# Left sums and weight sums of the second output projection as lanes of their own, ahead of the bias on VectorE

## The chip, the cores and the metric

The kernel runs on one core of a Trainium2 chip. The metric is the device time of one execution in microseconds; the time before is the median of 3 runs, 702.26 us (702.02 to 705.12). TensorE is PE in the profile, VectorE DVE, ScalarE ACT, GpSimd POOL; SP issues most transfers.

## The reference, cut to what matters

One decoder block in float32 on x of 2 x 512 x 1024 (two batches): causal attention with 32 query heads and 8 key heads, a product with a fake-quantised context, and a routed low-rank FFN, each with a layer norm in front and a residual around it.

```python
x = x + attn(layernorm(x))      # ... @ w_o.T + b_o, w_o 1024 x 1024
x = x + matmul(fake_quant(layernorm(x)), fake_quant(ctx))   # per batch, ctx 1024 x 1024
x = x + ffn(layernorm(x))       # x @ W_org.T + sum over e of coeff[e] * (x @ down[e]) @ up[e]
```

The change is in `out @ w_o.T + b_o` and the residual of the second batch.

## The kernel before

The whole kernel is one stream per engine, in the order in which the Python code records instructions. A program part is a generator: it records a few matmuls, yields, and in between `dispatch` lets VectorE and ScalarE record small steps ("hops") that wait in `lanes`. `dispatch` goes through the lanes by sorted name, so that a lane whose name begins with a lower number goes first, and takes a hop when its engine is not more than 0.6 us ahead of TensorE by a model of the clocks, and its inputs will be there. `force(key)` takes hops until the one with that key has been recorded. A recorded order is final: each engine runs its instructions in it and waits for what is not there yet.

The first part is attention for 2 batches x 8 groups of heads. Its pools (keys, queries, probabilities, and the PSUM banks of scores) are closed after the last group (`attn.close()`), and the space is given to a pool `tail` for the rest. Tiles of `tail` can be written once attention's last reader is done, which is the multiplication `oT` (L871) of the last group on VectorE.

At this point the rest begins: the four x tiles of batch 1 are loaded again (L273, 512 KB each, on SP), and a bias lane (4, "bias") adds b_o to each (L678, 128 x 1024).

The output projection of batch 1 is made by seven half-size products in place of eight, a Winograd form (`by_quarters`). With A the attention's output, B the weights wo, each cut into quarters, the products are called by numbers and run in the order 2, 1, 5, 6, 3, 7, 4:

- products 2 and 1 use quarters of A and B as they are. Product 2 is recorded beforehand, in the last steps of attention (`second_product`).
- product 5 is left sum `s_[0]` by the first weight sums `to1`; 6 is `s_[1]` by the second, `to2`; 3, 7 and 4 use later sums.
- the left sums are in a tile S (128 x 2 x 4 x 256): `s_[0]` = A(1,0) + A(1,1) and `s_[1]` = `s_[0]` - A(0,0) (`left_sums`, two instructions of 128 x 1024). After product 5 `s_[0]` is overwritten, after 6 `s_[1]`.
- the weight sums come from `right_sums`: four lists (first to fourth) of 4 instructions of 128 x 512 each, one for every k.

Each product is 2 PSUM banks of 4 matmuls of 128 x 512 in float32, which the profile counts as 16. What VectorE does with a result is `add` (L1335, x<-x,wo) and `gather` (L1253). `hooks` name what is to be recorded after a product.

Before the change, `left_sums` is the first hook of `rows_by_quarters`, so it is recorded when the projection starts; the weight sums are put in lane (1, "to") at the same place, in `output_by_quarters`. In the recorded order the four bias adds stand between `oT` and S.

What follows the projection of batch 1: `quantize_rows` (statistics L368, xn_b and a_b on ScalarE, L1026 and L1033), the transposes ta of a_b on TensorE (L1072), the base product of the FFN (wb, L1316, with sums tb and S again), cs (L958) and the context product ct (L969) of batch 1. Beside them the context of batch 1 is loaded in two buffers raw (L887), scaled on ScalarE (L910), bounded on VectorE (L914) and rounded on ScalarE (L918); the next load into a buffer is issued after the rounding. SP also issues the loads worg of the base weights (L1634) into the slots that wo's products have left. The last row tile of batch 0 runs in the same stretch: ct (L969, added at L975), st_c and xn_c (L368, L377), and its transposes tr_c on TensorE (L385).

Of the kernel before, what the change touches and what calls it, by code (L numbers as in the profile page):

```python
# [9 lines left out]
F32 = mybir.dt.float32  # L10
BF16 = mybir.dt.bfloat16
AF = mybir.ActivationFunctionType
ALU = mybir.AluOpType
AX = mybir.AxisListType

P = 128
B, S, D = 2, 512, 1024
# [5 lines left out]
NK = D // P  # L23
# [184 lines left out]
def kernel(  # L208
# [20 lines left out]
    nc = tc.nc  # L229
# [16 lines left out]
    def pool(name, bufs, on=stack, **kw):  # L246
        return Pool(on.enter_context(tc.tile_pool(name=name, bufs=bufs, **kw)), name, bufs)
# [5 lines left out]
    act = pool("act", 2)  # L253
# [18 lines left out]
    def load_x(dst, i):  # L272
        nc.sync.dma_start(dst, x[i * P : (i + 1) * P, :])  # L273
# [144 lines left out]
    def lane(name, *hops):  # L418
        lanes.setdefault(name, []).extend(hops)

    def take(name):
        hop = lanes[name].pop(0)
        if not lanes[name]:
            del lanes[name]
        hop.go()
# [17 lines left out]
    def force(key):  # L443
        while key not in done:
            name = next(n for n in sorted(lanes) if any(h.key == key for h in lanes[n]))
            hop = lanes[name][0]
            if hop.can and not hop.can():
                name = next(n for n in sorted(lanes) if not lanes[n][0].can or lanes[n][0].can())
            take(name)
# [54 lines left out]
    def take_xn():  # L504
        assert xn_free[0] > 0
        xn_free[0] -= 1

    def give_xn():
        xn_free[0] += 1
# [3 lines left out]
    xT, kTs, vs, qTs, wo = {}, {}, {}, {}, []  # L513
# [87 lines left out]
    def load_bo(name):  # L601
        t = xnp.tile([P, D], F32, tag="xn", name=name)
        nc.scalar.dma_start(t, bo.broadcast_to([P, D]))
        return t
# [72 lines left out]
    def add_bo(xi, bo_sb):  # L677
        nc.vector.tensor_tensor(xi, xi, bo_sb, ALU.add)  # L678

    def bias_lane(b, x_tiles, load):  # L680

        got = []

        def begin():
            take_xn()
            got.append(load())

        def add(t):
            add_bo(x_tiles[t], got[0])
            if t == NT - 1:  # L690
                give_xn()

        lane((4, "bias"), Hop("Activation", begin, can=lambda: xn_free[0] > 0))
        for t in range(NT):
            lane(
                (4, "bias"),
                Hop("DVE", lambda t=t: add(t), lambda t=t: [got[0], x_tiles[t]], key=("bias", b, t)),
            )
# [22 lines left out]
    stats, mT, invs, pts, oT = {}, {}, {}, {}, {}  # L721
# [446 lines left out]
    def load(key, deps, fn, chunks):  # L1168
        def run():
            w[key[0]] = fn()  # L1170
            made[key] = lambda: [w[key[0]](k) for k in range(chunks)]
            return iter(())

        unit(key, deps, run)
# [19 lines left out]
    sums = {}  # L1194
# [5 lines left out]
    def minus_(out_, a_, b_):  # L1200
        nc.vector.tensor_tensor(out_, a_, b_, ALU.subtract)

    def right_sums(quarter, shape, n, name):

        made = {}

        def of(t, k):
            return made[t][k // 2][:, k % 2, :]

        def two(t):  # L1210
            made[t] = [tail["t"](shape, f"{name}{t}_{i}") for i in range((n + 1) // 2)]

        def first(k):
            if k == 0:
                two(1)
            minus_(of(1, k), quarter(0, 1, k), quarter(0, 0, k))

        def second(k):
            if k == 0:
                two(2)  # L1220
            minus_(of(2, k), quarter(1, 1, k), of(1, k))

        def third(k):
            minus_(quarter(0, 1, k), quarter(1, 1, k), quarter(0, 1, k))

        def fourth(k):
            if k == 0:
                two(4)
            minus_(of(4, k), quarter(1, 0, k), of(2, k))

        makers = [[lambda k=k, f=f: f(k) for k in range(n)] for f in (first, second, third, fourth)]
        return makers, lambda t: lambda k: of(t, k)
# [71 lines left out]
    def left_sums(s_, a_):  # L1304
        nc.vector.tensor_tensor(s_[0], a_(1, 0), a_(1, 1), ALU.add)
        minus_(s_[1], s_[0], a_(0, 0))
        if len(s_) == 3:
            minus_(s_[2], a_(0, 0), a_(1, 0))

    def rows_product(name, b):  # L1310
        def product(p, l, r):
            n = NK // 2
            ps = [mm([P, 512], f"{name}{p}_{b}_{i}") for i in range(2)]
            for i in range(2):
                for k in range(n):
                    nc.tensor.matmul(  # L1316
                        ps[i], l[:, k, i * P : (i + 1) * P], r(k), start=(k == 0), stop=(k == n - 1)
                    )
                    yield 0.86
            return ps  # L1320

        return product

    def rows_by_quarters(name, b, lhs, weight, t_, hooks, ps2=None):


        n = NK // 2
        a_ = lambda i, j: lhs[:, (1 - j) * n : (2 - j) * n, i * 256 : (i + 1) * 256]
        b_ = lambda i, j: lambda k: weight((1 - i) * n + k)[:, j * 512 : (j + 1) * 512]

        product = rows_product(name, b)

        def add(i, j, h, src, first):
            xh = xs[b][2 * i + h][:, j * 512 : (j + 1) * 512]
            nc.vector.tensor_tensor(xh, xh, src, ALU.add)  # L1335

        if "S" not in sums:
            sums["S"] = act.tile([P, 2, n, 256], F32, tag="half", name="S")
        s_ = [sums["S"][:, i, :, :] for i in range(2)]
        more = tail["more"]([P, 2, 512], f"more{name}{b}")  # L1340
        hooks[0] = [lambda: left_sums(s_, a_)] + hooks.get(0, [])
        yield from by_quarters(product, a_, b_, s_, t_, [more[:, i, :] for i in range(2)], add, hooks, ps2=ps2)

    sums = {}
# [169 lines left out]
    def place_of(b):  # L1514

        if b:
            return lambda k: True
        return lambda k: ("v1" if k < 4 else ("k", 1, 1)) in done
# [4 lines left out]
    second_product = []  # L1523
# [86 lines left out]
    for t in range(NT):  # L1610
        xi = tail_x([P, D], f"x1_{t}")
        load_x(xi, NT + t)
        xs[1].append(xi)
    bias_lane(1, xs[1], lambda: load_bo("bo1"))
    rest = units[:]
    units.clear()
# [9 lines left out]
    def rows_quantised(i):  # L1626
        for t in (2 * i, 2 * i + 1):
            quantize_rows(1, t)

    def org_rows(i):  # L1630

        for k in range(i * NK // 2, (i + 1) * NK // 2):
            wk_ = ring_b([P, D], f"worg{k}")
            nc.sync.dma_start(wk_, worgT[k * P : (k + 1) * P, :])  # L1634
            org.append(wk_)

    def quarters_of(weight):
        return lambda i, j, k: weight((1 - i) * NK // 2 + k)[:, j * 512 : (j + 1) * 512]

    org = []  # L1640
    org_sums = []

    def sums_lane(makers, name, sources):

        for i, fns in enumerate(makers):
            for k, fn in enumerate(fns):
                key = {"key": (name, i)} if k == len(fns) - 1 else {}
                lane((1 if name == "to" else 2, name), Hop("DVE", fn, lambda k=k: sources(k), **key))

    def output_by_quarters():  # L1650
        of = quarters_of(lambda k: wo[k])
        makers, t_ = right_sums(of, [P, 2, 512], NK // 2, "to")
        sums_lane(makers, "to", lambda k: ())
        raws = [tail["raw"]([P, D], f"raw{i}") for i in range(2)]
        load_ctx(1, raws, place_of(1), lambda: None)
        hooks = {
            2: [lambda: force(("to", 0))],
            1: [lambda: force(("to", 0))],
            5: [lambda: force(("to", 1))],
            3: [lambda: rows_quantised(0), lambda: force(("to", 2)), lambda: org_rows(0)],  # L1660
            7: [lambda: force(("to", 3)), lambda: org_rows(1)],
            4: [lambda: rows_quantised(1)],
        }
        yield from rows_by_quarters("wo", 1, oT[1], lambda k: wo[k], t_, hooks, second_product)

    def base_unit(b):
        hooks = {}
# [33 lines left out]
    unit(("R2",), [("R1",)], g_route2)  # L1701
    made["R2",] = lambda: [coefs[b] for b in range(B)]
    unit(("W", 1), [("C", 0, t) for t in tiles] + all_of("W", 0), output_by_quarters)
    unit(("B", 0), [("W", 1)] + [("X", 0, t) for t in tiles], lambda: base_unit(0))
    unit(("B", 1), [("B", 0)] + [("X", 1, t) for t in tiles], lambda: base_unit(1))
# [68 lines left out]
```

## Time and profile before

| what | us |
|---|---|
| runs, median (lowest to highest) | 702.26 (702.02 to 705.12) |
| the profiled execution, its time | 703.59 |
| its span | 701.9 |
| TensorE busy | 678.7 (97%) |
| VectorE busy | 462.8 (66%) |
| ScalarE busy | 312.1 (44%) |
| chain that ended last: TensorE | 88% of the span |
| wo matmuls with sums (product 5) start to end | 443.42 to 452.25 |

The span is that of one execution as the profiler took it; its time has what lies around the span too. The chain that ended last is followed back from the last instruction, at each step to what released it. TensorE is busy in nearly every slice of the page, so the chain is mostly its own instructions, and the other engines stand in it where TensorE waits for them.

### The profile page before, as it was taken

The page shows a single profiled execution, that of the slowest core. Times are in us where ns is not written, and L with a number is a line of the kernel's source. Part 1 is how long each engine was busy: PE and PEld are TensorE (multiplying, and loading weights), DVE is VectorE, ACT ScalarE, POOL GpSimd, SP SyncE. Part 2 cuts the span into 40 slices and gives each one's busy share as a digit, 9 for nine tenths or more (in the row PEclk, how much of TensorE's full clock was granted, in tenths as well). Part 3 has the DMA queues.
Part 4 walks back from the last instruction along what each step waited for, and adds up shares of the span by engine and source line. Part 5 has one row for each costly group of instructions (what it writes and reads, how often), then busy time and mean ns, then how long its engine had stood idle before and what let it go on. Part 6 is the DMA issues. An engine that isn't in the chain of part 4 may idle for free.

```text
span 701.9 us, 9206 instructions
## 1 busy us (share of the span) xinstructions
PE 678.7 (97%) x3380; PEld 312.5 (45%) x3380; DVE 462.8 (66%) x1114; ACT 312.1 (44%) x694; POOL 83.1 (12%) x185
## 2 busy tenths in 40 slices
PE   6999999999999999999999989899999999999997
PEld 5654554343444444343434444344445454444443
DVE  5569745775676566374868664989869754724776
ACT  2025567786677657767777741228421000110100
POOL 3000011111211211121312230001000000000000
PEclk9999999999999999999999999999999999999999
DMA  8930100300130010000000006345100003000104
GB/s 276 337 84 1 31 1 0 103 19 1 33 115 35 31 60 31 1 1 1 1 1 1 2 1 212 118 158 203 59 2 0 1 30 120 0 0 0 61 0 180
DMA packets 24141, 40.58 MB, mean 58 GB/s; under 512 B 1824, under 2 KB 14240, under 8 KB 24096
## 3 DMA queue, kind: packets, MB, share of 16 engines
q1 hardware_dynamic: 23808, 38.95, 16.4%
q10 hardware_dynamic: 288, 1.05, 0.4%
q8 instruction: 26, 0.43, 0.3%
q14 instruction: 19, 0.16, 0.1%
HBM read 35.79 MB, written 4.19 MB: 57 GB/s over the span
## 4 chain that ended last, share of the span: by engine, by line
PE 88%; DVE 5%; ACT 4%; DMA 1%; issue 1%; POOL 0%; SPq 0%; DVEq 0%; ACTq 0%
PE pj_q L546 15%; PE wb L1316 14%; PE up L1398 7%; PE h L1362 7%; PE sc L748 6%; PE st L821 6%; PE wo L1316 6%; PE wo L969 6%; PE pv L862 5%; PE pj_k L546 4%; PE v L569 4%; PE ct L969 3%; ACT ms L770 3%; DVE ms L760 2%; DMA x<-in_x_dram 1%; PE st L829 1%
## 5 line engine op out<-in xcount | busy, mean ns | idle before, releaser
L770 ACT ACTIVATE ms<-ms,stats 128x512 f32<-128x512 f32 (+3 forms) x256 | 140.3, 549 | 85.0 <-DVE stats L760 84.9
L760 DVE CUSTOM_DVE_ANT_0 ms<-sc,mask 128x512 f32<-128x512 f32 (+3 forms) x256 | 115.4, 488 | 92.5 <-PE sc L748 80.5
L546 PE MATMUL pj_q<-xT,wq 128*128 128x512 f32 x256 | 120.5, 606 | 0.0
L838 ACT ACTIVATE pt<-st 128x1536 f32<-128x1536 f32 (+1 forms) x48 | 76.4, 1591 | 27.5 <-PE st L829 27.0
L841 POOL TENSOR_SCALAR_AFFINE_SELECT pt<-pt 128x512 f32<-128x512 f32 x64 | 43.1, 686 | 268.6 <-ACT pt L838 268.6
L546 PEld LDWEIGHTS pj_q<-xT,wq 128*128 128x128 f32 x256 | 45.1, 189 | 56.8 <-issue 55.7
L969 PE MATMUL wo<-wo,oT 128*128 128x512 f32 x128 | 61.8, 611 | 0.1
L821 PE MATMUL st<-qT,kT 32*128 32x128 f32 (+3 forms) x512 | 49.9, 467 | 6.2 <-DVE stats L760 5.9
L748 PE MATMUL sc<-kT,qT 32*128 32x128 f32 (+3 forms) x512 | 48.0, 467 | 1.1 <-ACT pt L838 1.1
L770 ACT ACTIVATION_READ_ACCUMULATOR ms<-ms,stats 128x1 f32 x256 | 47.8, 187 | 0.0
L862 PE MATMUL pv<-pt,v 128*32 128x128 f32 (+3 forms) x512 | 37.8, 436 | 0.0
L748 PEld LDWEIGHTS sc<-kT,qT 32*128 32x128 f32 x512 | 21.6, 183 | 33.7 <-ACT pt L838 16.1
L821 PEld LDWEIGHTS st<-qT,kT 32*128 32x128 f32 x512 | 20.1, 183 | 34.3 <-DVE stats L760 24.5
L969 PEld LDWEIGHTS wo<-wo,oT 128*128 128x128 f32 x128 | 22.2, 189 | 28.1 <-issue 27.2
L569 PE MATMUL v<-wv,xT 128*128 128x256 f32 x128 | 31.4, 394 | 0.0
L546 PE MATMUL pj_k<-xT,wk 128*128 128x512 f32 x64 | 29.5, 599 | 0.0
L969 PE MATMUL ct<-q,q1T 128*128 128x512 bf16 x128 | 29.3, 379 | 0.0
L1316 PE MATMUL wb<-tb,S 128*128 128x512 f32 x64 | 28.2, 596 | 0.0
L1316 PE MATMUL wb<-worg,S 128*128 128x512 f32 x64 | 28.0, 592 | 0.0
L1316 PE MATMUL wb<-worg,x3T 128*128 128x512 f32 x64 | 27.9, 593 | 0.0
L862 PEld LDWEIGHTS pv<-pt,v 128*32 128x32 f32 x512 | 15.0, 109 | 26.9 <-issue 23.2
L569 PEld LDWEIGHTS v<-wv,xT 128*128 128x128 f32 x128 | 24.2, 196 | 5.9 <-issue 2.4
(199 smaller groups left out, 918.9 us busy)
## 6 DMA issues: line engine op xcount, KB each, us to landing
wq<-in_wqT_dram SPq DMA_DIRECT2D x8, 512.0 KB, 8.8
ctx_raw<-in_ctx_dram SPq DMA_DIRECT2D x8, 512.0 KB, 3.4
wo<-in_woT_dram SPq DMA_DIRECT2D x8, 512.0 KB, 3.2
raw<-in_ctx_dram SPq DMA_DIRECT2D x8, 512.0 KB, 5.6
worg<-in_worgT_dram SPq DMA_DIRECT2D x8, 512.0 KB, 6.9
out_dram<-x SPq DMA_DIRECT2D x16, 256.0 KB, 2.1
x<-in_x_dram SPq DMA_DIRECT2D x7, 512.0 KB, 5.8
x_raw<-in_x_dram SPq DMA_DIRECT2D x4, 512.0 KB, 7.2
```

The source lines that it names most:

```text
L546: nc.tensor.matmul(ps, w(k), xT[b][k // 4][:, k % 4, :], start=(k == 0), stop=(k == NK - 1))
L569: nc.tensor.matmul(ps, xT[b][k // 4][:, k % 4, t * P : (t + 1) * P], wv(k), start=(k == 0), stop=(k == NK - 1),)
L748: nc.tensor.matmul(sc[:, s, part], qTs[b, c][row(s), t * P : (t + 1) * P], kTs[b][row(s), c // 4, :klen], start=True, stop=True,)
L760: nc.vector.tensor_tensor_reduce(out=ms[:, :klen], in0=sc[:, s, part], in1=mask[:, S - klen :], scale=-scale, scalar=BIG, op0=ALU.add, op1 ...
L770: nc.scalar.activation(ms[:, :klen], ms[:, :klen], AF.Exp, bias=least, scale=-1.0, accum_out=stats[g][:, t, s, 1:2],)
L821: nc.tensor.matmul(sc[:, s, part], kTs[b][row(s), c // 4, kb * P : (kb + 1) * P], qTs[b, c][row(s), kb * P :], start=True, stop=False,)
L838: nc.scalar.activation(pt, sc[:, :, :n], AF.Exp, scale=scale)
L862: nc.tensor.matmul(pv[row(s), kb * P :], vs[b][:, kb, h * HD : (h + 1) * HD], pt[:, s, part], start=(kb == 0), stop=(kb == NT - 1),)
L969: nc.tensor.matmul(ps, l[:, t * P : (t + 1) * P], r[:, cols], start=(k == 0), stop=(k == len(terms_) - 1))
L1316: nc.tensor.matmul(ps[i], l[:, k, i * P : (i + 1) * P], r(k), start=(k == 0), stop=(k == n - 1))
L1362: nc.tensor.matmul(ps[i], r(k)[:, i * P : (i + 1) * P], l[:, k, :], start=(k == 0), stop=(k == n - 1))
L1398: nc.tensor.matmul(ps[t], l[:, k, t * P : (t + 1) * P], r(k), start=(k == 0), stop=(k == n - 1))
```

## The change

The left sums and the weight sums of the output projection of batch 1 are put in lanes as soon as attention's pools are closed, before the bias lane is made. The left sums get a lane (0, "S") with two hops, one for each instruction, the second with the key "S1"; the first weight sums get the lane (1, "to") as before, but earlier. Both names sort ahead of (4, "bias"). S is allocated there too. `rows_by_quarters` makes the left sums itself only where the product has no second product made beforehand (that is, for the base products). The hook after product 2 forces "S1" and the first weight sums; the hook after product 1 is gone.

```diff
-        if "S" not in sums:
-            sums["S"] = act.tile([P, 2, n, 256], F32, tag="half", name="S")
         s_ = [sums["S"][:, i, :, :] for i in range(2)]
         more = tail["more"]([P, 2, 512], f"more{name}{b}")
-        hooks[0] = [lambda: left_sums(s_, a_)] + hooks.get(0, [])
+        if not ps2:
+            hooks[0] = [lambda: left_sums(s_, a_)] + hooks.get(0, [])
...
         xs[1].append(xi)
+    half = NK // 2
+    quarters_of = lambda weight: lambda i, j, k: weight((1 - i) * half + k)[:, j * 512 : (j + 1) * 512]
+    wo_makers, wo_t = right_sums(quarters_of(lambda k: wo[k]), [P, 2, 512], half, "to")
+    sums["S"] = act.tile([P, 2, half, 256], F32, tag="half", name="S")
+
+    def output_left(i):
+        s_ = [sums["S"][:, j, :, :] for j in range(2)]
+        a_ = lambda i, j: oT[1][:, (1 - j) * half : (2 - j) * half, i * 256 : (i + 1) * 256]
+        if i:
+            minus_(s_[1], s_[0], a_(0, 0))
+        else:
+            nc.vector.tensor_tensor(s_[0], a_(1, 0), a_(1, 1), ALU.add)
+
+    def sums_lane(makers, name, sources):
+
+        for i, fns in enumerate(makers):
+            for k, fn in enumerate(fns):
+                key = {"key": (name, i)} if k == len(fns) - 1 else {}
+                lane((1 if name == "to" else 2, name), Hop("DVE", fn, lambda k=k: sources(k), **key))
+
+    lane(
+        (0, "S"),
+        Hop("DVE", lambda: output_left(0), lambda: [oT[1]]),
+        Hop("DVE", lambda: output_left(1), key=("S1",)),
+    )
+    sums_lane(wo_makers, "to", lambda k: ())
     bias_lane(1, xs[1], lambda: load_bo("bo1"))
...
     def output_by_quarters():
-        of = quarters_of(lambda k: wo[k])
-        makers, t_ = right_sums(of, [P, 2, 512], NK // 2, "to")
-        sums_lane(makers, "to", lambda k: ())
         raws = [tail["raw"]([P, D], f"raw{i}") for i in range(2)]
         load_ctx(1, raws, place_of(1), lambda: None)
         hooks = {
-            2: [lambda: force(("to", 0))],
-            1: [lambda: force(("to", 0))],
+            2: [lambda: force(("S1",)), lambda: force(("to", 0))],
...
-        yield from rows_by_quarters("wo", 1, oT[1], lambda k: wo[k], t_, hooks, second_product)
+        yield from rows_by_quarters("wo", 1, oT[1], lambda k: wo[k], wo_t, hooks, second_product)
```

Because the order of all later instructions is recorded with the same model, it moves further on as well: on TensorE the transposes tr_c of the last row tile of batch 0 come before product 5 instead of after it; on VectorE the bias adds come between the sums and the adds of products 5 and 6; on ScalarE and SP the context's loads and steps come earlier against the row norms and the loads of worg; in the base product of batch 0, cs comes ahead of product 3, and product 7 after the context product.

More of the change, by code (lines that the diff above doesn't have):

```diff
@@ L1635, in org_rows @@
             org.append(wk_)
-    def quarters_of(weight):
-        return lambda i, j, k: weight((1 - i) * NK // 2 + k)[:, j * 512 : (j + 1) * 512]
     org = []
     org_sums = []
[L1643 to L1648, printed above, removed]
     def output_by_quarters():
-        of = quarters_of(lambda k: wo[k])
-        makers, t_ = right_sums(of, [P, 2, 512], NK // 2, "to")
-        sums_lane(makers, "to", lambda k: ())
         raws = [tail["raw"]([P, D], f"raw{i}") for i in range(2)]
```

## The prediction

> **What bounds the kernel now.** I read the page first: PE is busy 97% of the span and holds 88% of the chain that ended last, so only time in which TensorE stands still or runs slowly can be won. The waits of TensorE come next (who waited, for whom: us in total, times, longest):
>
> ```profile
> PE tr_a L385 <- DVE xn_a L377: 7.0, 1, 7.0
> PE st L821 <- DVE stats L760: 5.9, 10, 0.9
> PE wo L1316 <- DVE to L1201: 3.3, 1, 3.3
> ```
>
> The third line is the one in the stretch of the change. The chain of waits shows how it comes about (start, us, what):
>
> ```profile
> 427.95 0.70 DVE oT L871
> ...
> 429.65 5.83 DMA x<-in_x_dram
> 435.48 0.02 issue
> 435.50 1.23 DVE x L678
> 436.73 0.66 DVE x L975
> 437.39 1.13 DVE x L678
> 438.52 0.66 DVE x L975
> 439.18 1.19 DVE x L1335 x2
> 440.38 1.15 DVE S L1305
> 441.52 0.02 issue
> 441.55 1.23 DVE S L1201
> 442.77 0.61 DVE to L1201
> 443.38 0.04 issue
> 443.42 8.83 PE wo L1316 x16
> 452.25 0.88 PE tr_c L385 x8
> 453.13 27.47 PE wo L1316 x64
> ```
>
> VectorE ends oT at 428.65, then waits for the reloaded x, adds the bias, and only at 440.4 begins the left sums S. TensorE has finished its second product (p1) at 440.1 and waits to 443.42. And p5, 16 matmuls, takes 8.83 us there, where 64 later ones take 27.47, that is 6.87 for 16. The windows of TensorE say why (window, its length, PE busy with count, granted clock, DMA share, GB/s):
>
> ```profile
> 443.40:444.40 1.00, 0.98 (x3) 1.00 0.57 207
> 444.40:445.40 1.00, 1.00 (x3) 0.54 0.02 6
> 446.40:447.40 1.00, 1.00 (x2) 0.50 0.00 0
> 447.40:448.40 1.00, 1.00 (x3) 0.76 0.00 0
> 448.40:449.40 1.00, 1.00 (x3) 1.00 0.00 0
> ```
>
> One microsecond after the wait the granted clock falls to a half for 3.4 us. From 453 to 698 the chain is TensorE alone: an earlier p6 is an earlier end, if nothing else becomes late.
>
> **The change, part by part.**
>
> Removed and added: no matmul, no load, no VectorE sum is added or dropped. The 2 left sums and 16 weight sums are the same instructions, in lanes of their own. One x3T copy (0.69 on VectorE) goes to ScalarE (0.5); neither bounds. The cost of the parts is their new order.
>
> *Step 1, VectorE between oT and p5.* The program's order now is: S, S, two first sums, ct add, two first sums, ct add, two x adds of p2, the statistics of x_3, one second sum, xn_c. From 428.65: S 1.25 and 1.22 (S starts 440.29, 441.55, first sum 442.77); first sums 0.605 each (four in 2.42, starts); ct adds 0.66; x adds 0.605. After two sums 432.3, ct add 433.0, two sums 434.2, ct add 434.9 (its matmuls end at 433.1), x adds 436.1 (x_0 was there at 432.33 and x_1 at 433.5, when their bias adds began; the sums use oT and wo, long there). Then 1.31 + 0.24 + 0.15 for the statistics (437.8), GpSimd's power 1.05 (rstd ends 448.0, xn_c starts 449.05) with a second sum under it, xn_c 0.73: 439.6.
>
> *Step 2, TensorE.* The transposes tr_c of that xn_c now stand ahead of p5 instead of behind it. They can start at 440.12, when p1 ends; xn_c is 0.5 us early. They end at 441.0; S and the first sums have been ready since 434.2; p5 at 6.87 ends at 447.9, where p6 used to start at 453.13. This is 5.26 us: 3.31 of wait, 1.71 of half clock (half of 3.41), and 0.25 that I can't place and don't count. If the 0.5 us of cover in step 1 is gone, TensorE waits by what is missing, and p5 with it.
>
> The half clock goes with the gap if the gap causes it. For this speak the place (right behind the one idle of over 1 us after the start) and that idle of 0.9 us elsewhere had none. [...]
>
> *Step 3, what VectorE was doing in that time.* The four bias adds (1.14 each, 4.6 us) and the 0.61 sums are only shifted. Following the new order with the same durations: second sums end at 441.4 (p6 wants them at 447.9), third sums 445.0, fourth sums 447.5 (wanted at 461.6 and 468.5), the new S[0] at 449.8 (wanted by p3 at 454.7), then four x adds, bias 0 and 1 to 454.5, one context bound, S[1] at 456.3 (wanted by p7 at 461.6), the gathers of p6, bias 2 and 3 to 461.6. So VectorE is at p3's output when p3 ends (461.6), and the row norms start at 462.8, behind p3 by 1.2 us; before, by 0.8 (467.5 against 466.7). Cover on the tightest of these is 4.9 us; nothing here is priced.
>
> *Step 4, ScalarE and the SP queue.* Before, ScalarE scaled one context load of the second pair ahead of the row norms; now it takes four scalings and three roundings ahead of xn_b_0, and SP issues three of the raw loads ahead of the first worg load, and the fourth between worg 2 and 3. The in-order wait that this makes has been seen:
>
> ```profile
> 472.41 1.24 ACT L910 ACTIVATE raw<-raw,qp_sb,inv_s 128x1024 f32<-128x1024 f32 x1 [5.92 <-DMA raw<-in_ctx_dram]
> ```
>
> Behind such a wait stand xn_b_0, xn_b_1 (1.14 each) and a_b_0 (1.22), and TensorE's ta_0 waits for that. Let L be the landing time of a raw load (3.5 lowest, 5.6 median, 8.1 longest). First rounding done at 449.2; then three loads in a row, with 9.6 us of scaling, bounding and rounding between (1.13+0.60+1.05, 1.13+1.05, 1.13+2.28+1.22): a_b_0 at 458.8 + 3L. TensorE reaches ta_0 at 475.3. The last pair of raw loads in the trace, alone on the queue, landed in 4.0; loads queued with worg took to 6.7 (issued 465.63, used 472.41). Here the first two are nearly alone (DMA is idle from 444 on), the third stands behind three worg: 4 + 4 + 6.7 gives 473.5, a cover of 1.8 us. Bounds: 0 at L of 5.5 or less, 7.8 us of stall at 8.1. I take 0. ta_1 has less: p7 ends at 468.5, VectorE is free for it at 469.2, two gathers, four adds, a bound (7 x 0.605) and a_b_1 (1.22) give 474.7, against 475.8. The fourth worg load, held behind that raw load in the queue, lands by 468 to 471 and is read at 479; worg 4 to 7 are issued as p7 frees their slots, 466 to 469, and read from 483.
>
> *Step 5, behind 485.* The lanes' new state also moves p3 of the base product behind cs, p7 behind the context product. The matmuls are the same; TensorE needs at each place something that VectorE has: of these tr_c_1 is tightest, its xn_c some 0 to 0.6 us late by my durations, which come out late on the same stretch of before too (0.7 where the trace shows no wait). I take 0.2. From there the order is as before; xsum, which psq needs, hangs on the same VectorE work counted from the start of the base product and keeps its 0.5 us.
>
> Sum: 3.31 + 1.71 - 0.2 = 4.8. The profiled execution took 703.59 with a span of 701.9, 1.7 around it; its span becomes 697.1. I take the same 4.8 from the median of the runs, 702.26: 697.5.
>
> **The rivals.**
>
> *Gap without the clock.* The timed runs of before lie between 702.02 and 705.12, 3.1 apart, more than the 1.7 of one slow stretch: executions can differ by one, and the median, 1.3 under the profiled one, may not have had it. Against: the 1.3 may as well be what profiling costs, and the trace shown has the slow stretch. Then 702.26 - 3.31 + 0.2 = 699.15.
>
> *The gain is partly given back at ta_0, ta_1 or tr_c.* For: covers of 0.5, 1.8 and 1.1 us are small. A loss of 1 to 4 us leaves 698.5 to 701.5; 700 stands for it.
>
> *Slower: ScalarE behind the context loads* (step 4). All three loads at the trace's longest, 8.1: a_b_0 at 483.1, 7.8 us of stall at ta_0, 702.26 - 4.8 + 7.8 = 705.3. It decides against the change from a mean L of 7.1 us. Against: that long only loads took that shared the queue with several others, and two of these three don't.
>
> *It doesn't do what it says.* The lanes could have been filled later or S could wait for its slot. The built order has S right behind oT, and its slot was last read in the projections, so little remains: 702.3.
>
> **How the numbers follow.** Main case 0.56 (697.5; own range 696.8 to 698.3: 5.26 without any wait, 0.6 at tr_c_1 and 0.5 in step 1 against it), gap alone 0.24 (699.15), given back 0.10 (700), slower 0.06 (705.3), no effect 0.04 (702.3). Range: from 702.02 - 5.26 = 696.8 less a scatter of 0.5 to the gap alone with 0.6 of waits, 699.75, and the same small scatter: 696.3 to 699.9; slower, no effect and half of the given-back stay outside. 0.5% is 3.5 us, 698.75, and about what a measurement of this kernel tells from none: the gap alone is just within it. Faster: 0.56 + 0.03 of the given-back and 0.03 of the gap alone = 0.62; slower 0.06 and 0.01 of the rest = 0.07; same 0.31.
>
> **What would show it.** Right: no wait of wo for to, p5 in 6.9 us at a full clock, tr_c ahead of it at 440.1, p6 at 447.9 instead of 453.1, the base product's first matmul at 476.3 instead of 481.5. Step 1 wrong: a wait of tr_c for xn_c above 0.5. Step 4 wrong: a wait at ta_0 or ta_1 for a_b, with ScalarE idle before a raw scaling near 465. Step 5 wrong: waits of tr_c or wb between 500 and 547. The prediction is wrong if these together exceed 1.2 us, or if before's half clock turns out to be rare.

## The result and the profile after

| | median us | lowest to highest | executions |
|---|---|---|---|
| before | 704.35 | 702.02 to 707.52 | 12 |
| after | 700.47 | 699.03 to 701.68 | 12 |

The ratio is 0.9948, with a 95% interval of 0.9930 to 0.9965: 0.5% faster. The forecast of 697.5 is 0.9932 of its base of 702.26, inside that interval, but the time itself lies above the range of 696.3 to 699.9. The median of before over 12 executions is 2.1 us above the one over 3 that the prediction started from.

In the profiled execution of after the span is 698.2. These are TensorE's instructions in the stretch (timeline: start, us, engine, line, operation, out<-in, count, and in brackets the idle time before):

```profile
433.93 7.03 PE L1316 MATMUL wo<-wo,oT 128*128 128x512 f32 x16
440.79 1.04 PE L385 MATMUL tr_c<-ident,xn_c 128*128 128x128 f32 x8
441.67 13.90 PE L1316 MATMUL wo<-to,S 128*128 128x512 f32 x32
455.40 13.90 PE L1316 MATMUL wo<-wo,S 128*128 128x512 f32 x32
469.14 7.03 PE L1316 MATMUL wo<-to,oT 128*128 128x512 f32 x16
476.00 0.61 PE L1072 MATMUL ta<-identb,a_b 128*128 128x128 bf16 x8
476.93 0.62 PE L1072 MATMUL ta<-identb,a_b 128*128 128x128 bf16 x8 [0.32 <-ACT a_b L1033]
```

tr_c follows product 1 without a wait, products 5 and 6 take 13.7 us together (441.67 to 455.40), and the only new wait of TensorE is the last line, at the second group of ta. The clock beside it (windows: stretch, us, PE busy and count, granted clock, DMA share, GB/s):

```profile
441.70:445.10 3.40, 3.40 (x10) 1.00 0.89 330
445.10:448.50 3.40, 3.40 (x9) 1.00 0.02 6
```

No half clock is left where before had 0.50, and all 12 executions of after show a granted clock of 0.999 or 1.000. Two lines of ScalarE, and below them one of VectorE, show what the prediction had not seen (timelines of both, columns as above):

```profile
441.24 2.47 ACT L910 ACTIVATE raw<-raw,qp_sb,inv_s 128x1024 f32<-128x1024 f32 x2 [15.83 <-DMA raw<-in_ctx_dram]
443.61 1.05 ACT L1266 COPY morewo<-wo 128x512 f32<-128x512 f32 x2
```

```profile
444.21 1.29 DVE L1335 TENSOR_TENSOR x<-x,wo 128x512 f32<-128x512 f32 x2 [2.00 <-ACT morewo L1266]
```

VectorE stands still for 2.0 us at the adds of product 1: they wait for ScalarE's copies of that product, and these stand behind the scaling of two context loads that landed only at 441.

To compare profiles it helps to take stretches between the same instructions, from the timelines (us):

| profile | start to first K projection | oT (VectorE) to product 3 | ta to wb | wb to psq | last matmul's end to end of span |
|---|---|---|---|---|---|
| before | 26.40 | 31.88 | 1.07 | 83.73 | 3.77 |
| after | 27.23 | 26.61 | 1.39 | 83.91 | 4.06 |
| before again | 26.76 | 29.69 | 0.89 | 83.72 | 3.76 |
| after again | 27.36 | 26.62 | 2.63 | 83.90 | 4.06 |

All other stretches agree within 0.05 us. From oT to the end before took 273.9 (701.9 - 427.95) and after 269.4 (698.2 - 428.79): 4.5 us less. The spans differ by only 3.7, because after reached oT 0.84 later, and up to there the code is the same.

### The profile page after: what moved, and what is told of

It is laid out like the page before. It is cut to its first block, busy times and chain, and to the rows that moved or that the text cites. A ratio compares the mean times of both kernels' runs of the same rounds, so it can differ in the third digit from the quotient of the medians.

```text
span 698.2 us, 9188 instructions
## 1 busy us (share of the span) xinstructions
PE 676.4 (97%) x3366; PEld 312.6 (45%) x3380; DVE 462.4 (66%) x1113; ACT 312.6 (45%) x695; POOL 82.8 (12%) x185
## 4 chain that ended last, share of the span: by engine, by line
PE 81%; DVE 9%; ACT 5%; DMA 2%; issue 1%; POOL 0%; SPq 0%; DVEq 0%; ACTq 0%; POOLq 0%
PE pj_q L546 15%; PE wb L1316 14%; PE up L1397 7%; PE h L1361 7%; PE sc L748 6%; PE st L821 6%; PE pv L862 5%; PE wo L969 5%; PE pj_k L546 4%; PE v L569 4%; ACT ms L770 3%; PE ct L969 2%; DVE ms L760 2%; ACT pt L838 2%; PE tr_a L385 1%
## 5 line engine op out<-in xcount | busy, mean ns | idle before, releaser
L748 PEld LDWEIGHTS sc<-kT,qT 32*128 32x128 f32 x512 | 21.6, 183 | 33.7 <-ACT pt L838 16.1
L969 PEld LDWEIGHTS wo<-wo,oT 128*128 128x128 f32 x128 | 22.2, 189 | 28.1 <-issue 27.2
```

The costliest lines, as they stand in the source:

```text
L748: nc.tensor.matmul(sc[:, s, part], qTs[b, c][row(s), t * P : (t + 1) * P], kTs[b][row(s), c // 4, :klen], start=True, stop=True,)
L969: nc.tensor.matmul(ps, l[:, t * P : (t + 1) * P], r[:, cols], start=(k == 0), stop=(k == len(terms_) - 1))
```

## The experiments

**Before again.** No edit.

> The kernel before, unchanged, to see span and granted clock of every execution. [...] Rival B (the half clock is there in some executions only): a third or more of the executions show a clock of 0.999 to 1.000, and those are 1.7 us shorter than the rest. Ratio to itself 1.000 within 0.2%.

Median 703.62 (12 executions), ratio to the kernel before 0.9983 (0.9968 to 0.9997). Six of the twelve showed a granted clock of 1.000, six 0.997 or 0.998. The profile fell on one with 1.000. Its waits (engine, tile and line <- what ended the wait: us in total, times, longest) and its windows of TensorE:

```profile
PE wo L1316 <- DVE to L1201: 2.8, 1, 2.8
```

```profile
440.50:443.30 2.80, 0.01 (x1) 1.00 1.04 388
443.30:446.70 3.40, 3.39 (x8) 1.00 0.26 95
446.70:450.20 3.50, 3.50 (x9) 1.00 0.00 0
```

The gap is there, 2.8 us long, and no half clock behind it. So the half clock comes in some executions only, as the rival said. With the executions of before that ran beside the other experiments there are 64 with a clock on record:

| granted clock of the execution | executions | median us | lowest to highest |
|---|---|---|---|
| 0.999 to 1.000 | 14 | 702.73 | 701.62 to 703.73 |
| 0.996 to 0.998 | 39 | 704.57 | 702.83 to 706.08 |
| 0.994 | 11 | 707.44 | 705.93 to 707.87 |

In the profile of before the half clock behind the wait lasts 3.41 us (444.47 to 447.88). By that, one such stretch takes 0.24% off the mean clock, which makes 0.998; with a half clock behind the last matmul, where before's profile has another 1.4 us of it, 0.997. So about three in four executions have at least one, by this estimate. The border is not sharp: the profile of after with four matmuls at the start (below) has 0.998, and no wait of its TensorE is longer than 1.5 us. What the executions at 0.994 pay beyond one stretch is open, since none of them was profiled. The base of the prediction, 702.26, lies in the range of the first group and below every time of the others; its own clock is not on record.

**Left sums only.**

```diff
-    sums_lane(wo_makers, "to", lambda k: ())
     bias_lane(1, xs[1], lambda: load_bo("bo1"))
...
     def output_by_quarters():
+        sums_lane(wo_makers, "to", lambda k: ())
```

> Only the left sums go into their lane early; the weight sums are put in their lane where they were before. By durations the first weight sum is then ready at 437.8 on the clock of the trace of before, 2.3 us ahead of product 5, with two bias adds still in front of it. Theory A: no wait of wo for to, no half clock, tr_c behind product 5, a span 4.5 to 5.3 us below before, the same as the whole change within 0.5. Rival (the weight sums must be early too, or the bias must come last): a wait of 0.5 to 2 us ahead of product 5 and half or less of the gain.

Median 700.57 (6 executions, all at 1.000), ratio 0.9946 (0.9927 to 0.9965): within the intervals the whole gain. VectorE's timeline in this run:

```profile
432.75 1.22 DVE L1201 TENSOR_TENSOR S<-S,oT 128x1024 f32<-128x1024 f32 x1
434.93 1.23 DVE L678 TENSOR_TENSOR x<-x,bo 128x1024 f32<-128x1024 f32 x1 [0.96 <-DMA x<-in_x_dram]
...
436.73 1.21 DVE L678 TENSOR_TENSOR x<-x,bo 128x1024 f32<-128x1024 f32 x1
...
439.72 2.49 DVE L1201 TENSOR_TENSOR to<-wo 128x512 f32<-128x512 f32 x4
```

The first weight sum begins 3.0 us ahead of product 5 (442.76), with two bias adds still in front. What counts is that the left sums fill the time in which VectorE waits for x; the weight sums need not move. This run, too, has a wait at ta (2.24 from ta to wb).

**Left sums twice.**

```diff
-        hooks[0] = [lambda: left_sums(s_, a_)] + hooks.get(0, [])
+        hooks[0] = [lambda: left_sums(s_, a_)] * (2 if ps2 else 1) + hooks.get(0, [])
```

> The kernel before, with the two left sums of the output projection of batch 1 computed twice, so that the wait ahead of product 5 grows from 3.3 to 5.7 us. Theory A: half clock in every execution as before, span 2.4 us above before, ratio 1.0035. Rival B: the longer wait now brings the half clock always, where before it came in some only, so the median rises by 3 to 4 us, ratio 1.0045 to 1.006.

Median 713.28 (6 executions), ratio 1.0116 (1.0091 to 1.0141): more than either theory allowed. The wait is 6.1 us, and behind it (windows of TensorE):

```profile
446.80:450.20 3.40, 3.36 (x4) 0.50 0.00 0
450.20:452.70 2.50, 2.50 (x4) 0.50 0.00 0
452.70:456.00 3.30, 3.30 (x9) 1.00 0.00 0
```

This time the granted clock is 0.50 for 5.9 us (446.8 to 452.7). From oT to product 3 it takes 4.0 us more than before; another 5.2 come between wb and psq, where a transpose waits 3.2 us for xn_c and a granted clock of 0.51 follows (558.5 to 562.0). The longer model time has changed the recorded order there, so the run shows the clock, and does not isolate the gap.

**After, with matmuls at the start.** Four float32 matmuls that nobody reads, so that TensorE is busy before the first transposes.

```diff
+    warm = msp.tile([P, S], F32, tag="ms", name="warm")
+    nc.vector.memset(warm, 1.0)
+    warm_ps = ps_mm.tile([P, S], F32, tag="mm", name="warm_ps")
+    for _ in range(WARM):
+        nc.tensor.matmul(warm_ps, warm[:, :P], warm, start=True, stop=True)
+    clocks.catch_up()
+    clocks.at["PE"] = 0.0
```

> The kernel after, with four float32 matmuls of 128x512 on a tile of ones at the very start, in the 6.9 us in which TensorE waits for the first normed rows; their result is not used. If the spread of the executions comes from the clock of the first matmuls, TensorE is at full clock when the first transposes come: median 1 to 2 us below after, executions within 1.5 us of each other. If the spread comes from elsewhere (loads, for instance): median within 0.5 us of after, spread 2.6 us as there.

Median 700.86 (6 executions), spread 3.3 us: neither faster than after nor steadier. The four ended at 8.2, 1.2 us after the first transposes could have begun, yet the first K projection came at 25.92 instead of 27.23. This was given back: 0.65 us within attention, 0.9 at ta, 0.9 at the last store.

**After, context loads first.** Where the texts below speak of the third and fourth context load, they count from behind the first two.

```diff
         xs[1].append(xi)
+        if t == 1:
+            raws = [tail["raw"]([P, D], f"raw{i}") for i in range(2)]
+            load_ctx(1, raws, place_of(1), lambda: None)
...
     def output_by_quarters():
-        raws = [tail["raw"]([P, D], f"raw{i}") for i in range(2)]
-        load_ctx(1, raws, place_of(1), lambda: None)
```

> The kernel after, with the first two context loads issued behind the second of the four x loads instead of behind the fourth and wqf; every other instruction keeps its place. In the trace of after, VectorE stood 2.0 us at the adds of product 1, because ScalarE's copies of that product were queued behind the scaling of these loads, and TensorE then waited at ta_1 for a_b. Theory A (this chain makes the wait at ta_1, so the loss in step 4): no wait of VectorE for morewo, no wait of ta, ta to wb 0.9 us instead of 1.4 and more, a median 0.3 to 1.2 us below after. Rival (the wait at ta_1 comes from the fourth context load, queued with the worg loads): VectorE's wait goes, the wait of ta stays.

Median 699.69 (698.84 to 700.16), ratio 0.9930 (0.9910 to 0.9950); after, beside it on the same chip, had 701.33. ScalarE's timeline and, below it, the chain of waits (start, us, what ran):

```profile
437.99 2.44 ACT L910 ACTIVATE raw<-raw,qp_sb,inv_s 128x1024 f32<-128x1024 f32 x2 [12.27 <-DMA raw<-in_ctx_dram]
...
440.34 0.56 ACT L1266 COPY morewo<-wo 128x512 f32<-128x512 f32 x1
```

```profile
441.27 0.87 PE tr_c L385 x8
442.15 34.34 PE wo L1316 x80
476.48 0.89 PE ta L1072 x16
477.38 2.63 PE wb L1316 x6
```

The scaling starts 3.3 us earlier than in the profile of after and is done before the second half of product 1 is, so that VectorE's adds no longer wait for the copies; the chain is TensorE alone, and ta takes 0.89. The wait of VectorE and the wait at ta are both gone. This order is worth 1.6 us in the medians, and no execution of the one is as slow as the fastest of the other. But the fourth load comes earlier here too (its scaling starts at 467.05, in after at 468.11), so this run doesn't tell the two theories apart.

**The same, with three matmuls at the start.** As above, with `WARM = 3` and the scratch in a slot of rope and of the attention's output (`tag="sh"`, `tag="pv"`).

> As the run with the context loads first, with three float32 matmuls of 128x512 on a tile of ones at the very start (result not used), short enough to be done before the first transposes, in a slot that moves no other tile. If the clock of the first matmuls makes part of the level and spread of the executions: first K projection at 24.8 to 25.8 us instead of 26.4 to 29.2, median 1 to 2 us below the run without, executions within 2 us of each other. If the first part is bound by loads and VectorE: the same median within 0.5.

Median 698.98 (698.03 to 700.04), ratio 0.9923 (0.9901 to 0.9946), the best of all kernels run, though 0.7 below the one without is not beyond the intervals. First K projection at 25.14. The start of its TensorE (timeline; each float32 matmul counts as two):

```profile
1.50 4.40 PE L285 MATMUL warm_ps<-warm 128*128 128x512 f32 x6 [1.50 <-DVE warm L282]
6.98 1.11 PE L394 MATMUL tr_a<-ident,xn_a 128*128 128x128 f32 x8 [1.08 <-DVE xn_a L386]
```

The transposes take 1.11 where after took 1.97 for the same eight. Of the 2.4 us won here, 0.6 are lost within attention and 0.9 at the last store, as with four.

**Before, kept busy.** Four float32 matmuls that nobody reads, right ahead of product 5.

```diff
+        if ps2:
+            keep_busy()
         ps = yield from product(5, s_[0], t_(1))
```

> The kernel before, with four more float32 matmuls of 128x512 (result not used) right ahead of product 5, 3.4 us at full clock, so that TensorE is busy through the wait; no other instruction moves. Theory A (the gap costs 2.8 to 3.3 us, and the half clock another 1.7 in about three executions of four): no half clock, all executions at 0.999 to 1.000, median 1 to 1.8 us below before, and product 5 in 6.9 us from about the same start. Rival (the half clock doesn't come from the gap, or costs nothing on the path): same median as before within 0.5 us.

Median 702.68 (12 executions, all at 0.999 or 1.000), ratio 0.9969 (0.9955 to 0.9984). TensorE's timeline:

```profile
440.24 3.60 PE L1241 MATMUL idle<-wo 128*128 128x512 f32 x8
444.37 7.13 PE L1327 MATMUL wo<-to,S 128*128 128x512 f32 x16 [0.53 <-DVE to L1201]
```

Product 5 starts no earlier than without (16.1 us behind oT, 15.5 in before), and takes about 7 us instead of 8.83. The useless matmuls make the kernel 2.0 us faster in the medians (704.69 to 702.68), and the median is close to that of the 14 executions of before without a half clock (702.73). VectorE and ScalarE keep their order, instruction for instruction. So the half clock is a cost of its own, and the gap brings it.

**After again.** No edit.

> The kernel after, unchanged, beside the others on the same chip. Theory A: 3.5 to 4.5 us below before (ratio 0.994 to 0.995), clock 0.999 to 1.000 in all, ta to wb between 1.2 and 2.3 us, so that the wait at ta_1 is there again.

Median 701.33 (9 executions, 700.50 to 702.60), ratio 0.9957 (0.9941 to 0.9973), all at 0.999 or 1.000. The wait at ta is 1.6 this time, and the chain of waits shows how it comes about:

```profile
457.57 1.16 ACT q L918
458.72 0.02 issue
458.74 3.16 DMA raw<-in_ctx_dram
461.90 0.02 issue
461.93 1.24 ACT raw L910
463.17 1.05 ACT q L918
464.22 0.02 issue
464.23 5.41 DMA raw<-in_ctx_dram
...
470.81 1.23 ACT xn_b L1026
...
476.28 0.70 DVE xn_b L1029
476.98 0.02 issue
477.00 1.25 ACT a_b L1033 x2
478.25 0.05 issue
478.30 0.62 PE ta L1072 x8
```

Rounding, load, scaling, rounding, load: the fourth context load lands at 469.6, and xn_b, queued behind its scaling on ScalarE, is late.

**After, fourth scaling behind a_b_1.**

```diff
-                    Hop("Activation", lambda i=i: positive(i), lambda i=i: raw(i)),
+                    Hop(
+                        "Activation",
+                        lambda i=i: positive(i),
+                        lambda i=i: raw(i),
+                        lambda i=i: b == 0 or i != 5 or ("a1", b, 1) in done,
+                    ),
```

> The kernel after, with the scaling of the fourth context load taken on ScalarE behind a_b_1 instead of ahead of xn_b_0; the first two loads stay as late as in after, so VectorE still loses 1.5 to 2.2 us at product 1. Up to the transposes ta nothing else moves; behind them the base product's order shifts again, as the recorded model has it. Theory A1 (VectorE's lateness alone makes 0.3 to 0.5 us of the wait at ta_1, and the fourth load's landing the rest): ta to wb 1.2 to 1.4 us in the profile, between 0.9 of the run with the loads first and 2.6 of the last profile of after, and a median 0.3 to 1.3 us below after. Theory A2 (VectorE's lateness makes all of it): ta to wb 1.4 to 2.6, median as after. Theory A3 (the fourth load makes all of it): ta to wb 0.9.

Median 699.34 (698.13 to 702.10), ratio 0.9926 (0.9902 to 0.9949), ta to wb 1.19. Its waits, same columns as above:

```profile
ACT xn_b L1031 <- DVE off_b L1001: 4.8, 1, 4.8
...
DVE x L1340 <- ACT morewo L1271: 1.8, 1, 1.8
...
PEld L1077 <- ACT a_b L1038: 0.3, 1, 0.3
```

xn_b now waits for VectorE's statistics and not for a load; VectorE still loses 1.8 at product 1, and 0.3 us remain at ta. So in this profile the first theory holds: VectorE's lateness alone makes 0.3 us, and what goes beyond that (1.4 in the last profile of after) comes with the fourth load. The medians don't settle what that is worth: after did not run beside this kernel, and behind ta the recorded order differs too (wb to psq 83.72 against 83.90, last matmul's end to end of span 3.77 against 4.06), so 0.5 of the difference from after is not this wait.

## Why the prediction was wrong, point by point

**Bounds and gap (right).** The wait of 3.3 us and the half clock behind it are the cost, and the change removes both. From oT to product 3 after takes 26.61 where before took 31.88: 5.27 us, against 5.26 worked out in step 2. xn_c ended at 440.3 in after, 439.5 when both are counted from oT, against 439.6 worked out, and tr_c followed product 1 with no wait: step 1 holds.

**The half clock (right in cause, wrong in frequency).** It was counted as 1.71 in every execution. The run kept busy shows it as 2.0 in the medians, and the 64 executions show that 14 have none. The rival "gap without the clock" described these 14. That the executions of before differ by a half clock was thus seen, and given a chance of 0.24; the main case took all of them to have one.

**The base (the step that failed).** "I take the same 4.8 from the median of the runs, 702.26: 697.5." That median stood for three executions, two of them (702.02 and 702.26) in the range of the group without a half clock, and 1.71 of the 4.8 can't be won where it isn't paid. The profiled execution had it (1.3 us above that median, which the rival "gap without the clock" noted and set aside as a possible cost of profiling). The runs show that a time has the same 1.7 around its span with or without a half clock: 703.6 over 701.9, 701.6 over 699.9. From the profiled execution's own time the sum gives 703.59 - 4.8 = 698.8; from the median over 12, 699.55. Both lie inside the range that was stated, and the measured 700.47 is 0.9 above the second. Of the 3.0 us between 697.5 and 700.47, 2.1 are thus the base and 0.9 the gain. The rival "partly given back" names 700 and has 700.47 in its span, but that is luck in the main: it blames ta and tr_c for what was mostly the base. The upper end of the range is not its own sum either: 699.75 with the scatter of 0.5 that the lower end takes gives 700.25, not 699.9, and the measured time lies above that as well.

**Steps 3 and 4 (the rest).** "VectorE is at p3's output when p3 ends (461.6)": it got there at 464.24, 1.8 later when both are counted from oT, because the adds of product 1 wait for the copies on ScalarE, which the step left out. The cover of ta_1, worked out as 1.1, was less than that. ta_0 never waited, and its sum came out: a_b_0 ended at 474.3 in the profile of after again, 473.3 when counted from oT, against 473.5 worked out. For ta_1 step 4 had VectorE "free for it at 469.2". It doesn't speak of VectorE's own step on xn_b of the row tile before, which stands ahead of the gathers of product 7 and waits for ScalarE, there queued behind the fourth context load (timeline of VectorE, after again):

```profile
472.07 0.69 DVE L1029 TENSOR_SCALAR xn_b<-xn_b 128x1024 f32<-128x1024 f32 x1 [1.76 <-ACT xn_b L1026]
```

Step 4 put 0 on the wait at ta; the profiles show 0.3, 1.2 and 1.6 in three executions of the same code in this stretch, and the medians 1.6 with the loads put first. The chain was named (ScalarE behind the context loads), its price was taken at its lower bound. The sign that was named for it came: ScalarE idles 3.4 us ahead of the scaling at 468.11 in after. It did not make the kernel slower: the three loads in a row took 3.4, 3.2 and 5.4 in the profile of after again, far from three times 8.1.

**Step 5 (right).** 0.18 between wb and psq against 0.2 taken, and the waits there fit the cause that was named: the weight loads of tr_c wait for xn_c (0.29 and 0.34 in after, one wait of 0.17 in before).

Together in the profiled pair, from oT on: 5.27, less 0.32 at ta, less 0.18, less 0.3 behind the last matmul, for which the sum had no term, is 4.5, against 4.8 forecast. Between the medians 3.9 was won. How the rest splits is not shown: about one execution of before in five has no half clock to lose, and the wait at ta reached 1.6 in another profile of after.

## What to carry to other kernels

Before subtracting a cost that a profile shows from a median, check that the executions behind the median pay it: take the sum from the profiled execution's own time, and ask for the clock of the others. When one engine's work is pulled ahead, follow the first result that it then waits for back through the queue of the engine that makes it; here a copy of 0.5 us stood behind a load. A gap that is filled with useless matmuls, where nothing useful is at hand, is worth trying: here it gave 2.0 us where the change, beside it, gave 3.4.

## What the runs showed of the hardware

In the profile of before the wait of 3.3 us ahead of product 5 is followed by this (windows of TensorE, columns as above):

```profile
444.47:447.88 3.41, 3.41 (x6) 0.50 0.00 1
```

In left sums twice a wait of 3.2 us at tr_c has a clock of 0.51 behind it (558.5 to 562.0), and the wait of 6.1 us one of 0.50 for the 5.9 us shown. In before again a wait of 2.8 us has 1.00 behind it, and 14 of 64 executions of the same code show 0.999 or 1.000. What decides between the executions is not shown: of those of before, two were profiled, one with the half clock and one without.

The first matmuls are slow as well: the first eight transposes take 1.97 us in before and after, eight later ones 1.04. With four matmuls ahead of them they take 1.04, with three 1.11, and the four themselves take 6.75 us at the start, where four of the same size take 3.60 ahead of product 5 in the run kept busy. The record of the granted clock begins only at 11.0 us in before and at 12.7 in after (the windows' column reads 1.00 ahead of it), so that the clock makes the start slow is the author's estimate from these times. The first K projection comes at 25.1 with three matmuls at the start, at 25.9 with four, at 26.4 in before, 27.2 in after and 29.2 in left sums only. So part of the scatter between executions is made by then. It isn't all: with three matmuls the executions still lay 2.0 us apart.
